# Choosing for two tiles at once from tile 4 on instead of tile 8, and delaying the output products in one larger step

## The chip, the cores and the metric

The kernel runs on one core of one Trainium2 chip. The metric is the device time of one execution in microseconds. Beside it there is a trace of one profiled execution, with the start and length of the instructions on each engine: PE (TensorE, the matmuls), PEld (its weight loads), DVE (VectorE), ACT (ScalarE), POOL (GpSimd), and SP, which here only issues transfers.

## What is computed

The input `x` has 8 batches of 512 rows of 2048 numbers. All is in 32-bit floating point.

```python
# conditioned layer, one low-rank adapter per batch
c      = x @ W.T + b + 2.0 * (x @ A[adapter]) @ B[adapter]
# routed low-rank layer: the best of 8 experts, each of rank 16
logits = c @ route_w.T
h      = c @ A_e.T                       # for every expert, 8 * 16 = 128 numbers
h      = h * (one_hot(argmax(logits)) * max(logits))
out    = x + h @ Bw                      # 128 numbers -> 2048
```

`c` itself is never an output. So the kernel multiplies the weights first: `proj`, the 128 columns of the experts and the 8 of the router (136 columns together), is folded through `W`, and each batch's adapter is folded in on top of it. After that a row of `x` needs one product with a 2048 x 136 matrix, a choice, and one product of 128 x 2048.

## The kernel before

The rows are cut into 32 tiles of 128 rows, four to a batch; two neighbouring tiles make a pair, which is loaded, shuffled and stored in one buffer of five (`x_tiles`, `XB = 5`).

The first part (up to about 71 us) streams `W` and folds it with `proj` (L290). The second part is a loop over half tiles, `n` from 0 on, with `t, h = divmod(n, 2)`: tile `t`, half `h`. Every engine runs its own instructions in the order in which this loop writes them (the schedule is manual). So the order of the lines in one step is the order on each engine, and an instruction that waits holds up all that was written after it for that engine. A step `n` writes, in this order:

- `heads`, PE: half of the tile's product with the batch's matrix `m`, 8 of 16 column blocks (16 matmul records on line L482);
- `add_delta`, DVE (L654): the last output product of the step before is added onto `x` in place; a store is queued on SP when the tile is complete;
- `turn_x(t + 1, h)`, DVE (L237): the block transposes of the next tile's half, from the shuffled copy `xq`;
- `keep_heads` (ACT, L602) or `turn_moved` (DVE, L615): the last step of making `whT`, the transposed choice that an output product needs;
- in seven steps (`folds`: n = 5, 11, 19, 27, 35, 43, 51) `fold_adapter`: PE makes the adapter product of a later batch (L346), ACT copies it out (L567, L573), and DVE adds the constant part (L571); `add_c` on POOL finishes it two steps later (one for the first);
- `route`, DVE: bias, maximum, comparison and scaling, which give `wh`;
- `shuffle_slot(n)`, ACT and POOL (L253): four 32-partition copies that prepare the pair six steps ahead; ACT takes 2, 2, 3, 2 of them in the four steps of a pair and POOL the others;
- `move_heads`, POOL and ACT (L610): 16 small copies of `wh` for a pair, 9 on POOL and 7 on ACT;
- `delta`, PE (L648): an output product of one half tile, four matmuls of 512 columns into one buffer of two (`ps_o`);
- `turn_heads`, PE (L592): for a tile that is chosen for alone, a transpose of `wh` on PE;
- `load_x` of the pair five ahead, SP, two steps after the delta that completed a pair.

There are two ways from `ph`, the result of `heads`, to `whT`. Tiles below `NS` go alone: `route_one` on DVE, `turn_heads` on PE, `keep_heads` on ACT. Tiles from `NS` on go in pairs, except the last two: one `route` for both, `move_heads` on POOL and ACT, `turn_moved` on DVE, and no PE transpose. Pairs also put their results into PSUM banks that the single tiles use before (`pair_pool` closes the older pools).

Which deltas are due in a step is worked out ahead in the table `due`. Half tile `p` is due in step `p + lag`. A step with a fold has no delta, and the `lag` may grow there; if it does not grow, the next step has two deltas. With `lag` growing by 1 at n = 5, 11 and 19 it goes 3, 4, 5, 6 and stays at 6.

Of the kernel before, what the change touches and what calls it, by code (L numbers as in the profile page):

```python
# [18 lines left out]
def kernel(  # L19
# [240 lines left out]
    def turn_x(t, h):  # L260
        if t >= NT:
            return
        if h == 0:
            xT_tiles[t] = tpool.tile([P, NJ, P], F32, tag="t", name=f"xT_{t}")
        u, k = divmod(t, TPU)
        turn(xT_tiles[t], xq_tiles[u][:, k], h)
# [174 lines left out]

    NS = 8
    pools = {}

    def pair_pool(z):
# [17 lines left out]
    def place_heads(t):  # L465

        if t < NS:
            if t not in ph_tiles:
# [73 lines left out]
    def fold_adapter(b, t):  # L542
# [3 lines left out]

        if t < NS:
            lasts = [ps_s.tile([P, 512], F32, tag="s", name=f"pa_{b}_{k}") for k in range(2)]
# [33 lines left out]

    groups = [(t,) for t in range(NS)]
    groups += [(t, t + 1) for t in range(NS, NT - TPU, TPU)] + [(NT - 2,), (NT - 1,)]
    groups = {g[-1]: g for g in groups}

    def turn_heads(t):
        if t < NS - 1:
            pw = ps_s.tile([P, P], F32, tag="s", name=f"pw_{t}")
        else:  # L590
            pw = place_heads(t)[:, ds(NP, P)]
        nc.tensor.transpose(pw, wh_tiles.pop(t)[:, 0, :], ident)  # L592
        pw_tiles[t] = pw
# [7 lines left out]
    def keep_heads(t):  # L601
        nc.scalar.copy(new_whT((t,))[:, 0, :], pw_tiles.pop(t))  # L602
# [80 lines left out]
    folds = {8 * b + (3 if b else 5): b + 1 for b in range(B - 1)}.get  # L683
    adds_c = {8 * b + (5 if b else 6): b + 1 for b in range(B - 1)}.get

    lag, LAG = 3, 6
    due = {}
    done = 0  # L690
    for n in range(2 * NT + LAG):
        end = done if folds(n) else max(done, min(n - lag + 1, 2 * NT))
        due[n] = [divmod(p, 2) for p in range(done, end)]
        done = end
        if folds(n):
            lag = min(lag + 1, LAG)

    for n in range(2 * NT + LAG + 1):
        t, h = divmod(n, 2)
# [8 lines left out]
        turn_x(t + 1, h)  # L708
        if h == 1 and 0 < t <= NS:
            keep_heads(t - 1)  # L710
# [71 lines left out]
```

## Time and profile before

| | us |
|---|---|
| median of 3 runs | 316.72 (316.66 to 316.99) |
| profiled execution, device time | 316.97 |
| profiled execution, span of the trace | 315.2 |
| PE busy | 309.1 (98% of the span) |
| DVE busy | 230.2 |
| ACT busy | 189.5 |
| POOL busy | 187.4 |
| granted PE clock, mean | 0.997 |

The span goes from the first to the last instruction in the trace; 1.8 us of the device time lie outside it. A line of the timeline reads: start, length in us, engine, line of the kernel, operation, what it writes and reads, how many instructions were merged into it, and in brackets how long the engine had been idle before it and what ended that. Lengths of PE records overlap, since matmuls are pipelined; the time that a group of matmuls really takes is the distance from its start to the start of the next group.

### The profile page before, as it was taken

Reading aid. Unit: us, or ns where it says so; the run is one execution under the profiler, and the core shown is the slowest. Engines: PE = TensorE matmul, PEld = TensorE weight load, DVE = VectorE, ACT = ScalarE, POOL = GpSimd, SP = SyncE. Lnnn points to the kernel's source line nnn. Section 1 sums busy time; section 2 is a strip of 40 time slices with the busy share of each in tenths; the row PEclk is TensorE's granted clock in tenths of the full one; section 3 lists DMA queues with packets and bytes.
Section 4 is the critical chain, followed back from the end, with each engine's and each line's share of the span. In section 5 each row is a group of like instructions: output and inputs, shape, how many; then the busy total and the mean of one; then the engine's idle time right before and its main releaser. Section 6 shows DMA issues by size and latency. Waiting matters only on the chain.

```text
span 315.2 us, 5653 instructions
## 1 busy us (share of the span) xinstructions
PE 309.1 (98%) x2114; PEld 245.0 (78%) x2114; DVE 230.2 (73%) x390; ACT 189.5 (60%) x311; POOL 187.4 (59%) x284
## 2 busy tenths in 40 slices
PE   8999999999999999999999999999999999999994
PEld 7999999999777877777777768677767777777741
DVE  1010595937999798677988787888788887979684
ACT  2000133738799399559949983998499669912110
POOL 1011083979997866429884975698388929722220
PEclk9999999999999999999999999999999999999998
DMA  7999999989333957784877694848676876253467
GB/s 282 408 361 413 420 419 420 418 338 390 147 135 133 312 222 250 286 286 199 297 289 298 244 384 181 361 164 372 224 309 257 337 295 247 100 234 134 164 243 261
DMA packets 15595, 88.52 MB, mean 281 GB/s; under 512 B 1728, under 2 KB 4048, under 8 KB 5456
## 3 DMA queue, kind: packets, MB, share of 16 engines
q1 hardware_dynamic: 14400, 85.45, 68.9%
q0 software_dynamic: 320, 2.11, 1.6%
q10 hardware_dynamic: 848, 0.61, 0.6%
q8 instruction: 16, 0.26, 0.3%
q14 instruction: 11, 0.09, 0.1%
HBM read 54.60 MB, written 33.55 MB: 280 GB/s over the span
## 4 chain that ended last, share of the span: by engine, by line
PE 96%; DMA 2%; DVE 1%; DVEq 0%; issue 0%
PE ph L482 38%; PE po L648 33%; PE pc L290 19%; DMA pj<-in_proj_dram 2%; PE po L346 2%; PE pg L330 1%; PE ph L648 1%; PE ph L346 1%; PE pe_o L648 1%; DVE x L654 0%; PE pc L346 0%; PE pw L592 0%; DVE m L367 0%; DVEq L778 0%; PE pb L322 0%
## 5 line engine op out<-in xcount | busy, mean ns | idle before, releaser
L253 ACT COPY xq<-x 32x1024 f32<-32x1024 f32 x135 | 140.8, 1043 | 9.6 <-DMA x<-in_x_dram 4.8
L482 PEld LDWEIGHTS ph<-m,xT 128*128 128x128 f32 x1024 | 126.6, 190 | 25.4 <-issue 20.1
L253 POOL COPY xq<-x 32x1024 f32<-32x1024 f32 x121 | 125.5, 1037 | 22.8 <-DMA x<-in_x_dram 6.6
L482 PE MATMUL ph<-m,xT 128*128 128x136 f32 x1024 | 129.7, 280 | 0.3 <-DVE m L367 0.3
L648 PE MATMUL po<-fb,whT 128*128 128x512 f32 x240 | 111.8, 592 | 0.0
L654 DVE TENSOR_TENSOR x<-x,po 128x1024 f32<-128x1024 f32 x60 | 72.5, 1209 | 24.1 <-PE po L648 23.5
L237 DVE STREAM_TRANSPOSE xT<-xq 128x1024 f32<-128x1024 f32 x64 | 78.8, 1235 | 3.8 <-POOL xq L253 3.0
L648 PEld LDWEIGHTS po<-fb,whT 128*128 128x128 f32 x240 | 41.6, 190 | 31.6 <-issue 30.9
L290 PE MATMUL pc<-pj,w 128*128 128x136 f32 x512 | 59.9, 279 | 0.3 <-DMA pj<-in_proj_dram 0.3
L290 PEld LDWEIGHTS pc<-pj,w 128*128 128x128 f32 x512 | 59.5, 190 | 0.6 <-DMA pj<-in_proj_dram 0.6
L610 POOL COPY wq<-wh 32x64 f32<-32x64 f32 (+1 forms) x117 | 26.4, 226 | 54.0 <-DVE wh L534 40.9
L610 ACT COPY wq<-wh 32x64 f32<-32x64 f32 (+1 forms) x91 | 21.6, 238 | 21.3 <-DVE wh L503 10.0
L275 ACT COPY paced<-w 128x1 f32<-128x1 f32 x16 | 3.1, 191 | 39.7 <-DMA w<-in_w_dram 39.7
L276 DVE COPY paced<-w 128x1 f32<-128x1 f32 x16 | 2.4, 151 | 30.7 <-DMA w<-in_w_dram 30.6
L567 ACT COPY m<-ph 128x136 f32<-128x136 f32 x24 | 4.9, 284 | 26.7 <-PE ph L346 22.6
L578 POOL TENSOR_TENSOR m<-m,c 128x408 f32<-128x408 f32 x14 | 14.4, 1052 | 1.6 <-ACT m L573 1.1
L224 POOL COPY ad_q<-ad_ar 32x512 f32<-32x512 f32 x12 | 8.0, 668 | 10.0 <-DMA ad_ar<-in_cond_a_dram,arow_i 9.5
L388 POOL DMA_DIRECT2D bias_o<-in_bias_dram x1 | 0.7, 737 | 17.9 <-DVE bias_o L387 17.9
L571 DVE TENSOR_TENSOR m<-c,po 128x408 f32<-128x408 f32 x14 | 7.5, 576 | 4.0 <-PE po L346 3.9
L579 POOL TENSOR_TENSOR m<-m,c 128x544 f32<-128x544 f32 x7 | 9.4, 1343 | 0.0
L338 DVE TENSOR_TENSOR g<-pg,half 32x272 f32<-32x272 f32 x16 | 7.0, 437 | 3.2 <-PE pg L330 2.9
L615 DVE STREAM_TRANSPOSE whT<-wq 128x256 f32<-128x256 f32 (+1 forms) x13 | 5.2, 404 | 2.7 <-ACT wq L610 2.7
(81 smaller groups left out, 144.4 us busy)
## 6 DMA issues: line engine op xcount, KB each, us to landing
x<-in_x_dram SPq DMA_DIRECT2D x32, 1024.0 KB, 7.9
out_dram<-x SPq DMA_DIRECT2D x28, 1024.0 KB, 4.3
w<-in_w_dram SPq DMA_DIRECT2D x16, 1024.0 KB, 14.3
out_dram<-x SPq DMA_DIRECT2D x4, 512.0 KB, 2.6
out_dram<-x SPq DMA_DIRECT2D x6, 256.0 KB, 3.1
fb<-in_ffn_b_dram SPq DMA_DIRECT2D x1, 1024.0 KB, 17.5
pj<-in_proj_dram SPq DMA_DIRECT2D x2, 272.0 KB, 13.2
out_dram<-x ACTq DMA_DIRECT2D x1, 256.0 KB
```

What stands on the lines that cost most here:

```text
L224: copy(dst[:, :NQ], src[:, ts(q, NQ)])
L237: nc.vector.transpose(dst[:, ts(h, HJ), :].rearrange("p j (g t) -> p g j t", t=Q), src.rearrange("p g (j a) -> p g j a", a=Q)[:, :, ts(h, ...
L253: copy(xq_tiles[u][ts(i, Q), :, g, :].rearrange("p k (j a) -> p k j a", a=Q), src[:, :, :, i, :],)
L290: nc.tensor.matmul(pcs[z][:, n, :], w_tiles[oc][:, ts(j, P)], pj[:, oc, :], start=(oc == 0 and n == 0), stop=(oc == NO - 1), skip_group_ch ...
L346: nc.tensor.matmul(out, ad_q[ts(q, Q), b // 2, n, :], g4[ts(q, Q), b, :], start=start, stop=True, skip_group_check=not start, tile_positio ...
L482: nc.tensor.matmul(ph, xT_tiles[t][:, j, :], place(m, (j,))[:, 0, :], start=(j == 0), stop=(j == NJ - 1),)
L571: nc.vector.tensor_tensor(place(m, js), place(cs, js), banks[q], ALU.add)
L578: nc.gpsimd.tensor_tensor(place(m, js), place(m, js), place(cs, js), ALU.add)
L579: nc.gpsimd.tensor_tensor(m[1], m[1], cs[1], ALU.add)
L610: copy(wq[ts(i, Q), :, ts(q, Q)], wh[ts(q, Q), :, ts(i, Q)])
L648: nc.tensor.matmul(part, whT_tiles[t], fb[:, cols], start=True, stop=True)
L654: nc.vector.tensor_tensor(xs, xs, part, ALU.add)
```

## The change

`NS` becomes 4, so tiles 4 to 7 are now chosen for as the pairs (4, 5) and (6, 7) and no longer alone. The table of delays becomes explicit: the lag is 3 at first, 4 from the fold in step 5 on, and 6 from the fold in step 11 on. Step 12 then has no delta either, and the fold in step 19, at which the lag no longer grows, is followed by a step with two deltas. From step 20 on the same deltas are due in the same steps as before.

```diff
-    NS = 8
+    NS = 4
...
+    lags = {5: 4, 11: 6}
     lag, LAG = 3, 6
     due = {}
     done = 0
...
         end = done if folds(n) else max(done, min(n - lag + 1, 2 * NT))
         due[n] = [divmod(p, 2) for p in range(done, end)]
         done = end
-        if folds(n):
-            lag = min(lag + 1, LAG)
+        lag = lags.get(n, lag)
```

## The prediction

> **What bounds the kernel now.** I read the page's busy shares and slices first, then the list of waits, then the timeline of each engine around the folds of steps 11 and 19.
>
> ```profile
> PE 309.1 (98%) x2114; PEld 245.0 (78%) x2114; DVE 230.2 (73%) x390; ACT 189.5 (60%) x311; POOL 187.4 (59%) x284
> ...
> PE   8999999999999999999999999999999999999994
> ...
> PEclk9999999999999999999999999999999999999998
> ```
>
> PE is busy in every slice at the full clock. In the list of waits its stalls come to 1.7 us, none after 71.5 us. So the time is PE's own work: taking work off PE gains, moving work among the other engines gains nothing, and any wait put on PE after 71.5 us is lost for good. The question is whether some engine that now just keeps up will be late.
>
> The change moves tiles 4 to 7 onto the way that tiles 8 and 9 take now. So I read that way where the trace shows it: fold in step 19, pair (8, 9) routed in 19, moved in 20, turned in 21, its first delta in 22. PE in these steps:
>
> ```profile
> 134.59 2.02 PE L482 MATMUL ph<-m,xT 128*128 128x136 f32 x16
> 136.53 0.51 PE L346 MATMUL ph<-g,ad_q 32*128 32x136 f32 x8
> 136.87 0.87 PE L346 MATMUL po<-g,ad_q 32*128 32x136 f32 x24
> 137.67 2.12 PE L482 MATMUL ph<-m,xT 128*128 128x136 f32 x16
> 139.63 1.88 PE L648 MATMUL po<-fb,whT 128*128 128x512 f32 x4
> 141.34 2.02 PE L482 MATMUL ph<-m,xT 128*128 128x136 f32 x16
> 143.20 1.88 PE L648 MATMUL po<-fb,whT 128*128 128x512 f32 x4
> 144.91 2.02 PE L482 MATMUL ph<-m,xT 128*128 128x136 f32 x16
> 146.77 1.88 PE L648 MATMUL po<-fb,whT 128*128 128x512 f32 x4
> ```
>
> Start to start: heads 1.86 us (1.96 after a fold), a delta 1.72, a fold 1.14. ACT, DVE and the weight load in the same steps:
>
> ```profile
> 137.08 0.80 ACT L567 COPY m<-ph 128x136 f32<-128x136 f32 x4 [4.87 <-PE ph L346]
> 137.85 0.90 ACT L573 COPY m<-po 128x408 f32<-128x408 f32 x2
> 138.78 5.26 ACT L253 COPY xq<-x 32x1024 f32<-32x1024 f32 x5
> 144.06 1.76 ACT L610 COPY wq<-wh 32x64 f32<-32x64 f32 x7
> ```
> ```profile
> 145.92 0.45 DVE L615 STREAM_TRANSPOSE whT<-wq 128x256 f32<-128x256 f32 x1 [1.57 <-ACT wq L610]
> ```
> ```profile
> 146.66 0.30 PEld L648 LDWEIGHTS po<-fb,whT 128*128 128x128 f32 x2
> ```
>
> This is the row that decides. ACT cannot begin the fold's copies before PE's fold; behind them stand five shuffle copies (slots of steps 19 and 20), and only then its seven moves. `whT` is done at 146.37, which is 9.84 us after the fold began. PE asks for it at 146.66, after 10.13 us. The margin is 0.29 us, less a hand-over of about 0.05 (at 71.48 a DVE copy of `m` ends, at 71.53 the weight load that waited for it starts): 0.24 us. The ACT chain is fixed by its own work: at the fold of step 27 `whT` is done at 174.55, again 9.84 us after that fold's start at 164.71.
>
> **What the change removes from PE.** Four transposes, those of tiles 4 to 7, written in steps 10, 12, 14 and 16. The timeline around the first:
>
> ```profile
> 102.39 2.02 PE L482 MATMUL ph<-m,xT 128*128 128x136 f32 x16
> 104.24 1.88 PE L648 MATMUL po<-fb,whT 128*128 128x512 f32 x4
> 105.96 0.27 PE L592 MATMUL pw<-ident,wh 128*128 128x128 f32 x1
> 106.07 2.02 PE L482 MATMUL ph<-m,xT 128*128 128x136 f32 x16
> ```
>
> From the transpose's start to the next heads it is 0.11 us, though its record is 0.27 long. The Trainium skill (TensorE: Matmul & The Clock Gate, Part 4: PE-mode transpose) gives about 275 ns for such a transpose inside a kernel, from bf16; the record's 273 ns agrees as a length. As a price, four of them would be 1.10 us by the page and 0.44 by the distance of starts. In a full PE stream the distance counts, so I take -0.44. The page's figure would lower the sum below to +0.4, inside the bound.
>
> **What it does to the other engines.** DVE: four single choices of 1.6 us (122.58 to 124.17) go, two double ones of 2.15 (138.78 to 140.93) and two turns of 0.45 come: 1.2 us less. ACT: four copies of 0.27 go, 14 moves of 0.24 come: +2.3. POOL: 18 moves of 0.23, +4.1. Between the folds of steps 11 and 19 these three are busy 23.2, 21.2 and 15.8 us of 28.5, so the sums fit beside PE, and I cost them at nothing; only their order can hurt. SP issues the same transfers in the same order.
>
> **What it moves.** Deltas 7 to 13 come one step later. Step 12 has no delta, so up to step 19 PE's heads run 1.72 us earlier against everything that does not wait for PE; step 20 has two deltas and gives it back. Two deltas in one step are in the trace after the fold of step 27 (one run of eight from 167.81 to 171.24, 3.43 us, no gap), so step 20 costs nothing more.
>
> Now PE in the new order. The fold of step 11 starts at 108.02 now, at 107.91 without step 10's transpose. Then fold 1.14, heads(12) 1.96, heads(13) 1.86, delta(7) 1.72, and heads(14) to the weight load of delta(8) 1.75 (144.91 to 146.66): PE asks for the `whT` of tiles 4 and 5 after 8.41 us. The chain on ACT has the same members as at step 19: the fold's six copies, shuffle slots 11 and 12 with 2 + 3 copies (the trace of before shows these five directly behind the copies of this fold, from 110.26 to 115.52), seven moves, then the turn. It takes 9.84. DVE has the choice ready by about 112.3, before the moves at 115.4, and POOL's nine moves end near 114.7, so neither is last. The wait is 9.84 + 0.05 - 8.41 = 1.48 us. The moves, the turn and the delta do not show in tiles 4 to 7 now; their nearest row is pair (8, 9). From below, the wait would be nothing if the five shuffles stood elsewhere; from above I allow 1.9, for a weight load that refills an empty PE.
>
> Behind the waiting turn on DVE stands add_delta(7). It moves to about 117.75; before, it ran from 113.47. Its PSUM buffer is wanted back by delta(9) after 121, so PE does not feel it. The store of tile 3, and with it the load of pair 6, move by 4.3 us (see the third rival). The turns for heads(14) end near 113.6 against 114.6, those for heads(16) near 120.6 against 123, and `add_c` for batch 2 near 120 against 123: covered, by 1 us at the least. If a cover of 1 us is gone, the excess is lost one for one.
>
> **Sum.** -0.44 + 1.48 = +1.04 us. Against the profiled execution the span becomes 316.2 and its time, 1.8 more, 318.0. Against the median, which is 0.25 lower, 316.72 + 1.04 = 317.8.
>
> **The rivals.** A measurement can tell about 0.2%, or 0.63 us, from no change.
>
> Rival 1, not slower: the chain fits, because ACT gets through the fold's copies and slots earlier than at step 19. For it: ACT idles 2.0 to 2.7 us ahead of step 11's fold, and one copy (L602) goes there. Against it: that idle time is a wait for PE's fold, and the program order keeps the shuffles behind. Price: only -0.44, so 316.3. It decides once the chain is under 8.4 us instead of 9.84. With a stall under 1.07 us the whole is inside the bound too.
>
> Rival 2, the clock: PE stands still in mid-stream. The Trainium skill (TensorE: Matmul & The Clock Gate, the table under "Why this matters for your kernels") warns of gaps over about 3 us, after which the clock halves. The trace's only row is the 0.27 us gap at 71.5 us, with the clock still at 9 or more; no run here shows a gap of 1.5. By the rule 1.5 us costs no clock and the sum stays. If a window of about 3.4 us did run at half rate (an estimate from that page), it would add 1.7: 319.5.
>
> Rival 3, late `x`: pair 6 now comes 13.3 us after the store of tile 3 is issued (114.7 to 128.0), pair 7 likewise (128.8 to 142.1). In the new order these stores go out near 119.0 and 131.8, so the pairs land near 132.3 and 145.1, where ACT wants them near 130.6 and 147.3. ACT would wait 1.7 us for pair 6 and still be done before the fold of step 19 near 135.9. It decides if pair 6 lands after about 136.3; every us beyond is a PE stall in step 22. With a landing at 138 it adds 1.7: 319.5.
>
> **How the numbers follow.** The stall as worked: 0.72, from 317.2 to 318.2 (stall 0.9 to 1.9); about 0.05 of it lies inside the bound. Rival 1: 0.15 at 316.3. Rivals 2 and 3 together 0.10, near 319.5. For a gain beyond the bound I see no source, since the transposes are all that leaves PE: 0.03. The range has to take in rival 1 and the lower part of the other two: 316.2 to 319.0. Slower 0.77, same 0.20, faster 0.03.
>
> **What would show it.** Right: in the list of waits PEld or PE waits for `whT` (L615) once, for about 1.5 us, near 116.3 us; ACT's seven moves end near 117.2; the records of L592 fall from eight to four; step 20 has eight deltas in a row; from there on every PE record is about 1.0 us later than now. Wrong: no PE gap between 109 and 138 us (rival 1), PEclk below 9 in the slices after 116 us (rival 2), or a wait of ACT for `x` of more than 5 us near 131 us and a second PE gap near 147 (rival 3).

## The result, and the profile after

The changed kernel takes 317.84 us (median of 8 runs, 317.59 to 318.09) where the kernel before takes 316.74 in the same series: 1.10 us more, a ratio of 1.0031 with a 95% interval from 1.0022 to 1.0041. It is slower, by a third of a per cent. The forecast was 317.8.

The page of the changed kernel, busy shares and granted clock:

```profile
PE 308.3 (98%) x2110; PEld 244.3 (77%) x2110; DVE 228.8 (72%) x384; ACT 191.8 (61%) x321; POOL 190.9 (60%) x302
...
PEclk9999999999999999999999999999999999999999
```

PE is busy 0.8 us less, and the whole takes longer: there is a hole in PE that the busy sum does not show. Its list of waits (what waited, for what, us in total, times, longest) names it:

```profile
PE po L648 <- DVE whT L615: 1.3, 1, 1.3
```

The timeline of PE around it, from the heads and the fold of step 11 to the heads of step 15. The heads of steps 12 and 13 are one row of 32, since no delta lies between them:

```profile
105.69 2.02 PE L482 MATMUL ph<-m,xT 128*128 128x136 f32 x16
107.64 0.51 PE L346 MATMUL ph<-g,ad_q 32*128 32x136 f32 x8
107.98 0.87 PE L346 MATMUL po<-g,ad_q 32*128 32x136 f32 x24
108.78 3.97 PE L482 MATMUL ph<-m,xT 128*128 128x136 f32 x32
112.59 1.88 PE L648 MATMUL po<-fb,whT 128*128 128x512 f32 x4
114.31 2.02 PE L482 MATMUL ph<-m,xT 128*128 128x136 f32 x16
117.62 1.96 PE L648 MATMUL po<-fb,whT 128*128 128x512 f32 x4 [1.29 <-DVE whT L615]
119.41 2.02 PE L482 MATMUL ph<-m,xT 128*128 128x136 f32 x16
```

From the heads of step 14 (114.31) to those of step 15 (119.41) it is 5.10 us; an undisturbed step takes 3.57 (1.86 for the heads and 1.71 for the delta). So the hole costs 1.53 us. The 1.29 in brackets is shorter, because the recorded ends of matmuls overlap with what follows. ACT, DVE and the weight load in the same stretch:

```profile
108.19 0.80 ACT L567 COPY m<-ph 128x136 f32<-128x136 f32 x4 [4.87 <-PE ph L346]
108.96 0.90 ACT L573 COPY m<-po 128x408 f32<-128x408 f32 x2
109.89 5.26 ACT L253 COPY xq<-x 32x1024 f32<-32x1024 f32 x5
115.16 1.76 ACT L610 COPY wq<-wh 32x64 f32<-32x64 f32 x7
```
```profile
117.03 0.44 DVE L615 STREAM_TRANSPOSE whT<-wq 128x256 f32<-128x256 f32 x1 [2.71 <-ACT wq L610]
```
```profile
117.59 0.30 PEld L648 LDWEIGHTS po<-fb,whT 128*128 128x128 f32 x2 [1.47 <-issue]
```

It is the row of ACT work that the prediction read at the fold of step 19, with the same members: six copies of the fold, five shuffle copies, then the seven moves. `whT` is done at 117.47, 9.83 us after the fold began. The list puts the wait down to DVE, the last link; DVE itself had been idle for 2.71 us, waiting for ACT.

The two deltas of step 20 run without a gap (one row of eight records: a delta is two matmuls of 512 columns, and each shows as two records), and from there on the order is that of before:

```profile
138.73 3.60 PE L648 MATMUL po<-fb,whT 128*128 128x512 f32 x8
142.17 2.02 PE L482 MATMUL ph<-m,xT 128*128 128x136 f32 x16
```

The second row stands at 141.34 before: 0.83 us later. The profiled execution of the changed kernel was 0.27 us ahead already at the heads of step 9 (98.55 against 98.82), where the two kernels have done the same work, so the stage itself costs 1.10 us.

### The profile page after: what moved, and what is told of

It is laid out like the page before. It is cut to its first block, busy times and chain, and to the rows that moved or that the text cites. A ratio compares the mean times of both kernels' runs of the same rounds, so it can differ in the third digit from the quotient of the medians.

```text
span 316.0 us, 5666 instructions
## 1 busy us (share of the span) xinstructions
PE 308.3 (98%) x2110; PEld 244.3 (77%) x2110; DVE 228.8 (72%) x384; ACT 191.8 (61%) x321; POOL 190.9 (60%) x302
## 4 chain that ended last, share of the span: by engine, by line
PE 93%; ACT 3%; DMA 2%; DVE 1%; issue 0%; DVEq 0%; ACTq 0%
PE ph L482 36%; PE po L648 32%; PE pc L290 19%; DMA pj<-in_proj_dram 2%; ACT xq L253 2%; PE po L346 1%; PE pg L330 1%; PE ph L648 1%; PE ph L346 1%; PE pe_o L648 1%; ACT wq L610 0%; DVE x L654 0%; PE pc L346 0%; ACT m L573 0%; ACT m L567 0%
## 5 line engine op out<-in xcount | busy, mean ns | idle before, releaser
L610 POOL COPY wq<-wh 32x64 f32<-32x64 f32 (+1 forms) x135 | 30.4, 225 | 58.1 <-DVE wh L534 44.3
L610 ACT COPY wq<-wh 32x64 f32<-32x64 f32 (+1 forms) x105 | 25.0, 238 | 21.5 <-DVE wh L503 10.0
L615 DVE STREAM_TRANSPOSE whT<-wq 128x256 f32<-128x256 f32 (+1 forms) x15 | 6.1, 406 | 4.1 <-ACT wq L610 4.1
```

The source lines that it names most:

```text
L610: copy(wq[ts(i, Q), :, ts(q, Q)], wh[ts(q, Q), :, ts(i, Q)])
```

## The experiments

The theory: ACT's seven moves come too late, because they stand behind the fold's copies and five shuffle copies, and PE waits. Rival A: the larger delay is what costs, since PE runs ahead of everything that feeds it. Rival B: the way of a pair is too long in itself, over DVE's choice and POOL's nine moves. Rival C: a gap in PE also costs clock; it is rival 2 of the prediction, and its limit of 3 us and its 1.7 us are from there.

### The new delays alone

```diff
# on the kernel before, NS = 8
+    lags = {5: 4, 11: 6}
...
-        if folds(n):
-            lag = min(lag + 1, LAG)
+        lag = lags.get(n, lag)
```

> The kernel before (single tiles up to tile 7) with the new table of delays alone. Theory (the two-tile choice arrives late because ACT's seven moves stand behind the fold's copies and five shuffle copies): no pair is on the way in step 14, so PE has no gap, 316.7 us, within 0.2 of before. Rival A (the step without a delta is what costs: PE's heads run 1.72 us ahead of their suppliers in steps 12 to 19): the loss of 1.5 us stays, and the transposes are not saved, so 318.2 us.

Measured: 318.24 us against 316.91, ratio 1.0042 (1.0029 to 1.0056). By the time alone rival A has it exactly, and the theory misses. The timeline of PE in this run:

```profile
108.99 2.12 PE L482 MATMUL ph<-m,xT 128*128 128x136 f32 x16
112.37 0.30 PE L592 MATMUL pw<-ident,wh 128*128 128x128 f32 x1 [1.26 <-DVE wh L503]
112.50 2.02 PE L482 MATMUL ph<-m,xT 128*128 128x136 f32 x16
```

PE stands at one instruction: the transpose for tile 5, which only the single way has. In the kernel before, the delta of step 12 lies between the heads and this transpose; the new delays take that delta away, and PE arrives before DVE has made the choice (the weight load waits 1.43 us). DVE's last two instructions of that choice:

```profile
111.09 0.80 DVE L501 TENSOR_SCALAR rw<-key,win,top 128x8 f32<-128x8 f32 x1
111.93 0.29 DVE L503 TENSOR_TENSOR wh<-ph,rw 128x128 f32<-128x128 f32 x1
```

For the next tile the instruction of L501 takes 0.29, so 0.5 us of the wait is the length of this one instruction. The kernel before has it too (0.81 at 111.26), covered by the delta. So this is another wait than the changed kernel's, and that it is of nearly the same size is chance. The expectation had only thought of pairs. Whether running ahead costs in itself is not settled by this run, so the next one takes only this wait away.

### The new delays, with one transpose later

```diff
# on the kernel before with the new delays
         if t < NT:
             ...
             heads(t, h * HJ + HJ // 2, (h + 1) * HJ)
+            if n == 13:
+                turn_heads(5)
...
-        if h == 0 and 1 < t <= NS:
+        if h == 0 and 1 < t <= NS and n != 12:
             turn_heads(t - 1)
```

> The kernel before with the new delays, as in the run with the delays alone, but PE's transpose for tile 5 goes from the end of step 12 to after the heads of step 13. In the run with the delays alone PE stood 1.43 us at that transpose, which waited for the choice of tile 5 (L503), because the delta that covered it in step 12 was gone. If only that wait costs: heads(13) cover it, no gap, and the time is that of before, 316.9 us, within 0.2. If PE running ahead of its suppliers costs in itself, the loss shows up at another wait and the time stays near 318.2 us.

Measured: 316.78 against 316.79 us, ratio 0.9998 (0.9989 to 1.0007). PE:

```profile
109.36 3.97 PE L482 MATMUL ph<-m,xT 128*128 128x136 f32 x32
113.17 0.27 PE L592 MATMUL pw<-ident,wh 128*128 128x128 f32 x1
113.28 1.88 PE L648 MATMUL po<-fb,whT 128*128 128x512 f32 x4
```

No gap there, and none turned up elsewhere. Rival A falls: with the same delays PE is 1.72 us ahead in steps 12 to 19 and loses nothing, as long as no single consumer on PE meets its producer too early. That is shown here with single tiles; the run with two copies on POOL, further down, has the same delays with pairs and loses nothing either.

### Pairs with the old delays

```diff
# on the changed kernel
-    lags = {5: 4, 11: 6}
+    lags = {5: 4, 11: 5, 19: 6}
```

> The changed kernel with the old delays (lag 5 from step 11, 6 from step 19). Theory: PE asks for the choice of tiles 4 and 5 one step earlier, 6.57 us after the fold of step 11 begins instead of 8.42, and it is there after 9.95 us; the gap grows to 3.4 us, and the time is 316.74 - 0.44 + 3.4 = 319.7 us. Rival A (the delays cost): with the old delays the loss goes, 316.3 us. Rival C (the clock falls in a gap of over 3 us): up to 1.7 us more than the theory, 321.4 us, with a granted clock below 9 in the slice after the gap.

Measured: 322.65 us, ratio 1.0192 (1.0175 to 1.0209). The direction is the theory's and against rival A, but it is 2.95 us more than the theory's figure. PE:

```profile
117.67 2.66 PE L648 MATMUL po<-fb,whT 128*128 128x512 f32 x4 [3.15 <-DVE whT L615]
120.12 3.04 PE L482 MATMUL ph<-m,xT 128*128 128x136 f32 x16
123.00 1.88 PE L648 MATMUL po<-fb,whT 128*128 128x512 f32 x4
...
134.90 1.96 PE L648 MATMUL po<-fb,whT 128*128 128x512 f32 x4 [1.03 <-DVE whT L615]
```

Three things are to be seen. The gap is there, 3.3 us at the weight load. After it the same work takes longer: the delta 2.45 us instead of 1.72, the heads 2.88 instead of 1.86, together 1.75 more, with the granted clock at 0.50 between 119 and 122 us. That is rival C. And a second gap at 134.9, 1.2 us at the weight load, belongs to the pair (6, 7): it too is asked for a step early with the old delays, which the expectation had not counted. Together -0.44 + 3.3 + 1.75 + 1.2 = 5.8 us; measured are 5.7. So the larger delay does not cause the loss; it makes the loss smaller.

### Two shuffle copies from ACT to POOL

```diff
# on the changed kernel, in shuffle_slot
             na = 3 if k == 2 else 2
+            if n == 11:
+                na = 0
```

> The changed kernel, but the two shuffle copies that ACT makes in step 11 go to POOL, which idles 5.6 us there. Theory: ACT's chain is two copies of 1.05 us shorter, the choice is there 7.86 us after the fold's start, PE asks after 8.42, no gap: only the transposes remain, 316.74 - 0.44 = 316.3 us, faster than both kernels. Rival B (the way of a pair is too long in itself, over DVE's choice and POOL's nine moves, whatever ACT does before): the gap stays at 1 us or more, 317.3 to 317.8 us.

Measured: 316.39 us against 316.91, ratio 0.9985 (0.9976 to 0.9994): faster than before by 0.5 us (by the interval, 0.2 to 0.8), and faster than the changed kernel. ACT and DVE:

```profile
109.87 3.15 ACT L253 COPY xq<-x 32x1024 f32<-32x1024 f32 x3
113.03 1.76 ACT L610 COPY wq<-wh 32x64 f32<-32x64 f32 x7
```
```profile
114.89 0.45 DVE L615 STREAM_TRANSPOSE whT<-wq 128x256 f32<-128x256 f32 x1 [0.59 <-ACT wq L610]
```

Three copies instead of five ahead of the moves, and `whT` is done at 115.34. PE's delta begins at 116.14, and the list of PE's waits has no `whT` in it. What is left is the transposes' 0.44. Rival B falls: the way of a pair fits, if ACT comes to it in time.

### The moves ahead of the shuffle

```diff
# on the changed kernel, in the loop
+        if n == 12:
+            move_heads(groups[t - 1])
         shuffle(u, ms_u, ...)
-        if h == 0 and t > NS and t - 1 in groups:
+        if n != 12 and h == 0 and t > NS and t - 1 in groups:
             move_heads(groups[t - 1])
```

> The changed kernel, but in step 12 ACT makes its seven moves before its three shuffle copies; no engine does more or less work. Theory: ACT takes up the moves when the choice is there (about 4.4 us after the fold's start), POOL's nine moves then end last at about 6.9, the turn at about 7.4, PE asks after 8.42: no gap, 316.3 us. Rival B (the way of a pair is too long in itself): the gap stays, 317.3 to 317.8 us. A rival to the sum of the transposes: if they cost their record's length, 0.27 us each, this and the run with the copies on POOL give 315.6 us.

Measured: 317.06 us against 316.91, ratio 1.0005 (0.9996 to 1.0014). The gap is gone as the theory says, yet only part of the gain is there. PE and DVE of this run:

```profile
116.21 1.88 PE L648 MATMUL po<-fb,whT 128*128 128x512 f32 x4
...
127.31 1.98 PE L648 MATMUL po<-fb,whT 128*128 128x512 f32 x4 [0.23 <-DVE x L654]
```
```profile
119.28 1.25 DVE L237 STREAM_TRANSPOSE xT<-xq 128x1024 f32<-128x1024 f32 x1 [3.15 <-ACT xq L253]
```

Delta(8) at 116.21 is on time. Three steps on, delta(11) waits for its PSUM buffer, 0.43 us at the weight load, and delta(12) another 0.16 with no releaser named. (DVE ends the turn of pair (6, 7) at 130.99, 0.12 us before that weight load, so it is probably that turn.) The buffer is freed by add_delta(9) on DVE, and DVE is late. From 119.28 to 130.99, over add_delta(9) and the turn of pair (6, 7), it works without a pause. It had stood 3.15 us at `turn_x(8, 0)`, waiting for ACT's two shuffle copies of step 13. These stand where they stood before, behind the same amount of ACT work, while PE now comes 1.5 us sooner. In the run before this one ACT had two copies less to do, and DVE waited only 0.57 us there. Behind that start DVE loses time once more, in the choice of pair (6, 7):

```profile
123.57 0.82 DVE L530 TENSOR_TENSOR key<-key,rank 128x16 f32<-128x16 f32 x1
124.62 0.84 DVE L532 TENSOR_TENSOR key<-key,win 128x16 f32<-128x16 f32 x1
126.05 1.21 DVE L654 TENSOR_TENSOR x<-x,po 128x1024 f32<-128x1024 f32 x1
```

The same two instructions take 0.18 and 0.17 for pair (4, 5), so they cost 1.3 us here. That is more than either wait, so the waits needed both: the late start and the two long instructions. No run takes the long instructions away alone.

From start to start, steps 17 and 18 take 0.50 and 0.23 us more than 3.57. Together that is 0.73 us; this run lies 0.67 us above the one before it, and 0.59 above the expected 316.91 - 0.44.

### More copies ahead of the moves

One more shuffle copy on ACT in step 12, and in the other run one more each in steps 11 and 12, taken from POOL:

```diff
# on the changed kernel, in shuffle_slot
             na = 3 if k == 2 else 2
+            if n == 12:              # the other run: n in (11, 12)
+                na += 1
```

> The changed kernel with one more shuffle copy on ACT, in step 12, taken from POOL. The gap grows by 1.05 us to 2.6 us. If the clock stays in a gap of this length: 317.84 + 1.05 = 318.9 us, with gap and time still growing one for one. If the clock falls here as it did with two more copies (a gap of 3.6 us, 2 us on top): up to 320.7 us.

> The changed kernel with two more shuffle copies on ACT, one each in steps 11 and 12, taken from POOL. Theory: the chain ahead of the seven moves grows by two copies of 1.05 us, one for one: the gap goes from 1.5 to 3.6 us and the time from 317.84 to 319.9 us. Rival B (the way over DVE and POOL decides): no change, 317.8 us. Rival C (the clock falls in a gap of over 3 us): up to 1.7 us more, 321.6 us, with a granted clock below 9 in the slice after the gap.

Measured with two more: a median of 321.86 us against 317.00 (ratio 1.0159, 1.0131 to 1.0188), six runs from 320.06 to 323.60. With one more: 320.69 us against 316.79 (ratio 1.0099, 1.0077 to 1.0122), two runs at 318.79 and 318.94 and four from 320.65 to 320.86. The theory alone gives 319.9 and 318.9. One run of the first kernel (320.06) and two of the second lie within 0.2 us of that; the others are longer. PE with two more copies:

```profile
119.75 3.07 PE L648 MATMUL po<-fb,whT 128*128 128x512 f32 x4 [3.40 <-DVE whT L615]
122.62 2.63 PE L482 MATMUL ph<-m,xT 128*128 128x136 f32 x16
```

And PE with one more, in windows of 1 us (columns: busy time of PE, PEld, DVE, ACT and POOL with their records, then the granted clock, the share of the DMA engines and GB/s):

```profile
119.00:120.00 1.00, 1.00 (x2) 0.55 (x3) 0.91 (x1) 0.99 (x2) 1.00 (x1) 0.64 0.00 0
120.00:121.00 1.00, 1.00 (x2) 0.33 (x1) 0.52 (x1) 0.97 (x2) 0.94 (x2) 0.50 0.32 131
121.00:122.00 1.00, 1.00 (x2) 0.33 (x1) 0.73 (x1) 0.99 (x2) 0.96 (x2) 0.50 0.94 393
122.00:123.00 1.00, 1.00 (x6) 0.81 (x5) 0.57 (x1) 0.99 (x2) 0.96 (x2) 0.66 0.99 401
123.00:124.00 1.00, 1.00 (x11) 1.00 (x10) 1.00 (x2) 0.99 (x2) 0.96 (x2) 1.00 0.30 123
```

The gap grows by the copy's time, one for one: 1.47, 2.52 and 3.57 us at the weight load with none, one and two more. That is the theory's dose, and rival B again has no place for it. On top comes the clock: it is at half from shortly after the gap's end for a little over 3 us. The delta and the heads behind the gap together take 1.76 us more than 1.72 + 1.86 in both traces, and 1.75 with the old delays above. With one more copy the four runs with a mean clock of 0.992 or 0.993 lie 1.9 us above the two with 0.998 and 0.999. With two more, four runs lie 1.7 to 2.1 us above 319.9, and two (322.87 and 323.60, mean clock 0.988) about 1 to 2 us higher still; neither of those was profiled, so what they lost is not known.

### The price of a transpose

```diff
# on the kernel before, in turn_heads
+        nc.tensor.transpose(pw, wh_tiles[t][:, 0, :], ident)
         nc.tensor.transpose(pw, wh_tiles.pop(t)[:, 0, :], ident)
```

> The kernel before with each of the eight PE transposes of a choice made twice, into the same place. If a transpose costs the distance of starts (0.11 us), this adds 8 x 0.11 = 0.88 us: 317.6 us. If it costs the length of its record or the page's figure (0.27 us), it adds 2.2 us: 318.9 us.

The "page" is the one that the prediction names for its transposes.

Measured: 317.84 against 317.00 us (ratio 1.0032, 1.0022 to 1.0042), 0.84 us for eight, 0.105 each. PE:

```profile
84.41 0.27 PE L592 MATMUL pw<-ident,wh 128*128 128x128 f32 x1
84.52 0.27 PE L593 MATMUL pw<-ident,wh 128*128 128x128 f32 x1
84.63 2.02 PE L482 MATMUL ph<-m,xT 128*128 128x136 f32 x16
```

Each record is 0.27 long, and the next starts 0.11 after it. In a PE stream without gaps the distance is the price.

## Why the prediction was right, point by point

- The bound: right. PE was full, and what was put on it as a wait after 71.5 us was never made up.
- The transposes: -0.44 was right. Doubling eight of them gives 0.105 us each, and the run with two copies on POOL, where nothing but the transposes is left, is 0.5 us faster; its interval of 0.2 to 0.8 leaves out the 1.09 that four records of 0.27 would give. With that price the forecast would have been about +0.4, too little to tell from no change.
- The wait: forecast 1.48, measured 1.53. Without the wait PE would have asked 1.75 us after the heads of step 14, at 116.06, which is 8.42 us after the fold's start (forecast 8.41; the stretches that the prediction lists add up to 8.43, which makes no difference). ACT's row takes 9.83 (forecast 9.84). The only term that was mis-sized by more than 0.02 is the hand-over from DVE to the weight load: taken as 0.05, it was 0.12 (117.47 to 117.59). With it the sum is 1.53 - 0.44 = +1.09; measured are +1.10.
- What is late next: right in part. add_delta(7) ran at 117.40 (forecast 117.75), the other turns were on time and step 20 cost nothing. But the reserve behind them was thinner than the prediction says: the run with the moves first shows that the wait in step 14 covered a further lateness of DVE, about 0.6 us of which comes out once the wait is gone. The prediction put the choice of a pair at 2.15 us; that of pair (6, 7) took 3.5 (122.57 to 126.09).
- Rival 1 (the chain fits) did not come about in the changed kernel, but its point of decision holds: with `whT` at 7.7 us after the fold's start instead of 9.83 there is no gap.
- Rival 2 (the clock): the prediction left it out of its sum, and rightly for this kernel: none of its 8 runs went above 318.09, and the granted clock in its trace is 1.00 from 108 to 126 us. The ground given was too comfortable. The limit of about 3 us (the Trainium skill, TensorE: Matmul & The Clock Gate, the table under "Why this matters for your kernels") would have cleared a gap of 2.5 us as well, and four of six runs with such a gap lost clock. The changed kernel lies 1.05 us below that. The price of 1.7 us was right: 1.75 and 1.76 in the three traces that show it.
- Rival 3 (late `x`): did not come about. The two loads of pair 6 were issued from 122.66 to 123.0 and took at most 6.9 us, so the pair was there by 129.9 instead of 132.3; the list of waits from 105 to 150 us has no wait for `x`.

The prediction costed the missing delta of step 12 by what it does to the pairs alone. That step is also what a single tile's transpose had been covered by, and on single tiles it costs as much.

## What to carry to other kernels

When an engine is full and the others only have to be in time, find the row in the trace where the new order already exists, and compare two numbers counted from the same event: when the full engine will ask, and when the last link of the chain delivers. Where they cross, look at what stands ahead of the chain on the slowest link, since an engine with time to spare can still deliver late (ACT was busy 23.8 of the 28.0 us between the folds of steps 11 and 19); here two copies of 1 us, given to an idle neighbour, turned a loss of 1.1 us into a gain of 0.5. A time that fits a theory is not yet the theory's wait: the delays alone gave the rival's time, by another instruction.

## What the runs showed of the hardware beyond the expectation

A PE gap of 1.47 us cost only itself in all 8 runs. One of 2.5 us cost 1.9 us more in four of six runs, and the trace of one of these shows the granted clock at half for a little over 3 us. Gaps of 3.3 and 3.6 us did so in all 5 and in 5 of 6 runs, by their times and mean clocks. So the same program has times 2 us apart and more. What decides for a gap of 2.5 us in a single execution no run here shows.

Some of DVE's short instructions took several times as long as others of the same line. In the changed kernel it cost nothing, but the waits in the runs with the delays alone and with the moves first hold it. From the choice of pair (6, 7) in the changed kernel, with POOL beside it:

```profile
123.44 0.90 DVE L530 TENSOR_TENSOR key<-key,rank 128x16 f32<-128x16 f32 x1
124.38 0.17 DVE L531 TENSOR_REDUCE win<-key 128x2 f32<-128x16 f32 x1
124.58 0.84 DVE L532 TENSOR_TENSOR key<-key,win 128x16 f32<-128x16 f32 x1
```
```profile
120.06 5.33 POOL L253 COPY xq<-x 32x1024 f32<-32x1024 f32 x5
```

The last two of POOL's five copies end at 124.31 and 125.39, and L530 and L532 end 0.03 us after them, at 124.34 and 125.42. It is so throughout this trace: L530 runs 13 times; in six it starts during such a copy, takes 0.73 to 0.90 us and ends 0.02 or 0.03 us behind the copy, and in the other seven it takes 0.17 or 0.18. L528, L529 and L531 start during a copy 13 times in all and never take longer than 0.18; L528 and L529 read `ph` in PSUM, and L531 has a single input, where L530 and L532 read two from SBUF. So it looks as if such an instruction waits until POOL's copy is through. No run was made to test this.
